# An eight-image convolution, attention and scan program: convolutions placed singly amid two attentions, scans at one pace, last layers three images behind

## The chip, the core and the metric

The kernel runs on one core of a Trainium2 chip. The metric is the device time of one execution in microseconds, the median of several runs. The core's engines each have an instruction queue of their own, worked through in order: TensorE (PE, matrix multiplication), VectorE (DVE), ScalarE (ACT), GpSimd (POOL) and SyncE (SP, which here only issues transfers). PE writes to PSUM, which has eight banks of 512 32-bit columns on 128 partitions; everything else lies in SBUF, and longer-lived data in HBM.

## What is computed

Eight images of 256 channels and 32 x 32 positions, in 32-bit floats, pass through four layers with residual connections, each on normalised input:

```python
x = x + attention(group_norm(x))            # layer 0: 8 heads of 64, l2-normalised q and k
x = x + conv3x3(group_norm(x)) * s1 + b1    # layer 1
x = x + conv3x3(group_norm(x)) + b2         # layer 2
x = x + mixer(group_norm(x))                # layer 3
```

The mixer of layer 3 normalises over channels and sends four groups of 64 channels through a selective scan: a short convolution, projections, then for each of 128 channels and 16 states the recurrence

```python
h = dA_t * h + dBu_t          # 1024 steps
y_t = sum over states of C_t * h
```

Then come a gate, depthwise and pointwise convolutions, a second attention (8 heads of 32), a projection `fc`, layer norms, GELU, a depthwise 3x3 convolution and a last projection. Images don't depend on each other; within an image the layers follow in order.

## The kernel before

A channel takes a partition, so an image is two tiles of 128 x 1024. The program is unrolled Python; each image is cut into pieces that are generators, and what a generator yields is a planned cost. A list scheduler then fixes the order in each engine's queue from the order of the program, from dependencies and from planned durations. Once built, the order doesn't change. PE, DVE and ACT instructions pass through a recording helper, so the profile shows all of them under line L105 and they are told apart by their tiles; POOL's have lines of their own (L974, L1005, L1006).

The pieces of one image:

- *front attention* (`front_attention`): loads x, normalises it (`xn`), makes `v`, `q` and `k`, and works through 64 units. A unit is two score matmuls into a `big` PSUM tile (two banks, two buffers), one exponential on ACT (`p`), and two matmuls of `p` with `v` into `acc`. DVE adds up the `p` tiles (`p<-p`) for the softmax denominators.
- *convolutions* (`front_convs`): the output projection `wout` of the attention, then two times `conv3x3`, 72 matmuls of 512 columns each from the padded images `im`; the result of both halves of a channel tile gathers in one `big` tile. The weights come in 24 transfers of 192 KB (12 for each convolution), issued from ACT's queue into six shared buffers.
- *scan* (`scan_layers`): normalisation, then for each of four groups a front (`branch_front`: projections into the PSUM tile `da`, short convolution on `raw`, step sizes `dt` and `du` written to HBM and read back spread out), 16 units of scan (`scan_steps`) and an end (`branch_back`). A unit is: POOL multiplies `du` by B (`hs<-du,bc`, L974); ACT makes two decays of 512 columns (`da<-dt,a_neg`, one PSUM bank each, two buffers); DVE runs two scans (`hs<-da,hs`); POOL multiplies by C (L1006); PE sums over states (`y<-hs,sel`).
- *back layers* (`back_layers`): the gate, two projections with depthwise convolutions, and the second attention, again 64 units, without DVE's additions. Its results go to HBM as `mix`.
- *ending* (`back_out`, `back_end`): reads `mix`, the projection `fc`, layer norm, GELU, the depthwise convolution (`dw`, 16 DVE instructions), a layer norm, the last projection, and adds the stored `xd`.

A program-level loop sets what runs beside what. Image 0's front attention and convolutions come first, alone. Then round b runs the scan of image b beside the "dense" work: the back layers of b-1, the front attention of b+1, and then the convolutions of b+1 with the ending of b-1 woven in at listed places. Round 0 has no back layers and round 7 no front and no convolutions; after round 7 come back layers and ending of image 7. `interleave` lets the scan take a step each time the dense work's planned cost has passed another `pace`:

```python
    for cost in dense:
        spent += cost or 0.0
        while scans is not None and due <= spent:
            due += pace
            with held():
                if next(scans, END) is END:
```

The pace is 1.8 in round 0, 2.78 in rounds 1 to 6 and 1.6 in round 7. Two steps make a unit of scan. The front attention's costs are multiplied by 0.35 (`slow`), so few scan steps fall into it, and `lull` puts fewer into parts of the convolutions. Under `held()` each scan instruction gets an ordering edge to the last dense instruction of its engine, so the scheduler can't pull it forward. A last block, reached only if a check of the softmax sums fails, computes everything anew by another path; it doesn't run.

Of the kernel before, what the change touches and what calls it, by code (L numbers as in the profile page):

```python
# [19 lines left out]
P = 128  # L20
# [13 lines left out]
def preact_stack(ctx: ExitStack, tc: tile.TileContext, I, out, cols):  # L34
# [16 lines left out]
    ps_acc = ctx.enter_context(tc.tile_pool(name="ps_acc", bufs=1, space=PSUM))  # L51

    xmp = ctx.enter_context(tc.tile_pool(name="xmp", bufs=4))
    mp = ctx.enter_context(tc.tile_pool(name="mp", bufs=3))
    hsp = ctx.enter_context(tc.tile_pool(name="hsp", bufs=6))
    dtp = ctx.enter_context(tc.tile_pool(name="dtp", bufs=2))
    bcp = ctx.enter_context(tc.tile_pool(name="bcp", bufs=4))
    ps_da = ctx.enter_context(tc.tile_pool(name="ps_da", bufs=2, space=PSUM))
# [3 lines left out]
    xdp = ctx.enter_context(tc.tile_pool(name="xdp", bufs=3, space=DRAM))  # L62
# [16 lines left out]
    def xm_tile(name):  # L79
        return xmp.tile([P, TP], F32, tag="xm", name=name)  # L80
# [4 lines left out]
    def tiles(xt):  # L85
        return [xt[:, t] for t in range(2)]

    def load_x(src):
        xt = xp.tile([P, 2, N], F32, tag="x", name="xt")
        nc.sync.dma_start(out=xt, in_=src)  # L90
        return xt
# [146 lines left out]

    images = [wp.tile([P, TW], F32, name="im%d" % t) for t in range(2)]
    raw = wp.tile([P, N + 4], F32, name="raw")  # L240
    for t in images + [raw]:
        nc.gpsimd.memset(t, 0.0)
# [45 lines left out]
    def group_stats(mv, psum):  # L288

        with urgent():  # L290
# [11 lines left out]
            rs = sp.tile([P, 2], F32, tag="rs", name="rs", bufs=4)  # L302
# [4 lines left out]
            shift = sp.tile([P, 2], F32, tag="shift", name="shift", bufs=4)  # L307
# [73 lines left out]
    BY_HALF = tuple((h, da_tile) for h in HALVES)  # L381
# [43 lines left out]

    def project_both(name, srcs, evac):

        last = len(srcs) - 1
        w = [chunk(name, m) for m in range(2)]
        ps = [big_tile() for _ in range(2)]  # L430
        for k, src in enumerate(srcs):
            for m in range(2):
                for h in range(2):
                    tensor.matmul(
                        ps[m][:, HALVES[h]],
                        w[m][:, k],
                        src[:, HALVES[h]],
                        start=k == 0,
                        stop=k == last,
                    )  # L440
                if k == last:
                    evac(m, ps[m])
            yield 4 * 0.86
# [168 lines left out]
    def front_attention(src, img, exact=False):  # L612
        xt = img["x"] = load_x(src)
        yield 0
        mv = stats_tile()
        for t in range(2):
            channel_stats(mv, t, xt[:, t])
        xn = [work("xn0"), work("xn1")]
        group_norm(tiles(xt), group_stats(mv, big_tile), [t[:, 0:N] for t in xn])
# [134 lines left out]
    def conv3x3(xt, mv, name, bname, evac):  # L754
# [4 lines left out]
            tiles(xt), group_stats(mv, acc_tile), [t[:, 1:33, 1:33] for t in im], image  # L759
        )  # L760
        mv = stats_tile()
        for m in range(2):
            scalar.activation(xt[:, m], xt[:, m], AF.Identity, bias=col(bname, m))
        yield 1
        for m in range(2):
            ps = big_tile()
            n = 0
            for c in range(2):
                for dy in range(3):
                    w = chunk(name, (m * 2 + c) * 3 + dy)  # L770
                    for dx in range(3):
                        for h in range(2):
                            tensor.matmul(
                                image(ps[:, HALVES[h]]),
# [5 lines left out]
                        n += 1  # L780
                    if n < 18:
                        yield 5.2
# [5 lines left out]
    def front_convs(img):  # L788
# [19 lines left out]
        def evac_2(m, ps):  # L808
            vector.tensor_add(xt[:, m], xt[:, m], ps)
# [877 lines left out]
```

## Time and profile before

| what | value |
|---|---|
| median of 3 runs | 6551.4 us (6540.02 to 6552.56) |
| the profiled execution, its time | 6534.17 us |
| its span, granted clock | 6532.5 us, 0.91 |
| PE busy | 5503.0 us, 84% |
| DVE busy | 4003.1 us, 61% |
| POOL busy | 2737.3 us, 42% |
| ACT busy | 2701.2 us, 41% |
| convolution matmuls `big<-im,w` | 1104.0 us busy |
| scans `hs<-da,...` on DVE | 1024 instructions, 1265 ns and 1209 ns mean |
| decays `da<-dt,a_neg` on ACT | 1024 instructions, 686 ns mean |
| POOL L974 and L1006 | 512 each, 2636 ns and 2547 ns mean |
| transfers | 495.99 MB, mean 76 GB/s |

A line of a group names what is written and what is read, the shape, the count, busy time and mean, then the engine's idle time just before these instructions and what ended it. A matmul here shows as two records. Lines on waits have the waiting engine and tile, what it waited for, the total in us, the number of waits and the longest. The clock is a share of full speed, as granted to PE.

### The profile page before, as it was taken

What the parts mean: (1) busy time and instruction counts of PE and PEld (TensorE: products, weight loads), DVE (VectorE), ACT (ScalarE), POOL (GpSimd) and SP (SyncE); (2) the same over time, 40 slices, a digit from 0 to 9 for tenths busy, and PEclk for the clock granted to TensorE, in tenths of its full rate; (3) what the DMA queues carried; (4) which work ended last, traced back from release to release, by engine and by line L of the source; (5) the groups of instructions that cost most, each with busy time, mean ns of one, the idle gap of its engine ahead of it and who ended that gap; (6) DMA issues with size and microseconds to landing.
All of it is one profiled execution on the core that took longest, in us unless ns stands there. A gap on an engine that the chain in (4) does not pass through costs nothing.

```text
span 6532.5 us, 52259 instructions
## 1 busy us (share of the span) xinstructions
PE 5503.0 (84%) x17318; PEld 1846.7 (28%) x17318; DVE 4003.1 (61%) x4613; ACT 2701.2 (41%) x3241; POOL 2737.3 (42%) x1302
## 2 busy tenths in 40 slices
PE   8886688899888988989889898899889898876496
PEld 2331133223332233222332233322332223311222
DVE  5247845577556775567756776567855777555622
ACT  3223424644255532644236442555326442344242
POOL 0006653634435353543517345263435435276500
PEclk9997889999899989999899998999899998988697
DMA  1022232323233132321223222231323212233301
GB/s 44 26 62 76 78 89 76 88 74 88 69 91 98 39 93 77 101 85 57 81 82 99 75 75 80 83 103 44 91 77 101 87 57 82 77 82 88 97 26 43
DMA packets 224761, 495.99 MB, mean 76 GB/s; under 512 B 61016, under 2 KB 102616, under 8 KB 223456
## 3 DMA queue, kind: packets, MB, share of 16 engines
q1 hardware_dynamic: 168032, 419.12, 22.2%
q10 hardware_dynamic: 56448, 73.43, 3.9%
q8 instruction: 139, 2.28, 0.1%
q14 instruction: 142, 1.16, 0.1%
HBM read 411.09 MB, written 72.88 MB: 74 GB/s over the span
## 4 chain that ended last, share of the span: by engine, by line
PE 53%; DVE 24%; issue 6%; DMA 6%; ACT 6%; POOL 4%; SPq 1%; ACTq 0%; DVEq 0%; POOLq 0%
PE big L105 33%; PE acc L105 11%; DVE hs L105 6%; PE da L105 5%; DVE p L105 4%; DVE dw L105 3%; POOL hs L1006 3%; PE y L105 3%; DVE u L105 2%; DVE t L105 1%; DMA du_m<-a 1%; POOL hs L974 1%; ACT p L105 1%; ACT da L105 1%; DMA dt<-dt_m 1%
## 5 line engine op out<-in xcount | busy, mean ns | idle before, releaser
L974 POOL TENSOR_TENSOR hs<-du,bc 128x1024 f32<-128x1024 f32 x512 | 1339.7, 2636 | 1623.2 <-DMA du<-du_m 683.0
L1006 POOL TENSOR_TENSOR hs<-hs,bc 128x1024 f32<-128x1024 f32 x512 | 1303.7, 2547 | 1027.7 <-DVE hs L105 841.2
L105 ACT ACTIVATE p<-big 128x1024 f32<-128x1024 f32 x1024 | 1038.5, 1021 | 735.0 <-PE big L105 724.2
L105 PE MATMUL acc<-p,v 128*64 128x512 f32 x4096 | 1151.8, 636 | 8.8 <-ACT both L105 6.0
L105 ACT ACTIVATE da<-dt,a_neg 128x512 f32<-128x512 f32 x1024 | 684.2, 686 | 1144.7 <-DVE hs L105 442.1
L105 PE MATMUL big<-im,w 128*128 128x512 f32 x2304 | 1104.0, 631 | 20.4 <-ACT im L105 20.4
L105 DVE TENSOR_TENSOR p<-p 128x1024 f32<-128x1024 f32 x448 | 720.0, 1607 | 295.2 <-ACT p L105 201.8
L105 DVE TENSOR_TENSOR_SCAN hs<-da,carry,hs 128x512 f32<-128x512 f32 x512 | 623.5, 1265 | 256.4 <-ACT da L105 176.0
L105 DVE TENSOR_TENSOR_SCAN hs<-da,hs 128x512 f32<-128x512 f32 x512 | 599.7, 1209 | 286.6 <-ACT da L105 267.6
L105 PE MATMUL big<-qk,qk 64*128 64x512 f32 x2048 | 647.9, 663 | 95.2 <-ACT p L105 85.5
L105 PE MATMUL y<-hs,sel 128*32 128x512 f32 x2048 | 454.0, 674 | 315.3 <-POOL hs L1006 314.8
L105 PE MATMUL big<-q,k 64*128 64x512 f32 x2048 | 616.8, 660 | 107.2 <-ACT p L105 60.6
L105 PEld LDWEIGHTS big<-im,w 128*128 128x128 f32 x2304 | 446.9, 201 | 689.5 <-issue 642.1
L1005 POOL COPY carry<-hs 128x2 f32<-128x2 f32 x256 | 104.2, 407 | 823.0 <-DVE hs L105 745.0
L105 PEld LDWEIGHTS acc<-p,v 128*64 128x64 f32 x4096 | 213.7, 137 | 820.3 <-issue 719.0
L105 PEld LDWEIGHTS big<-qk,qk 64*128 64x128 f32 x2048 | 178.2, 192 | 537.1 <-issue 280.1
L105 PEld LDWEIGHTS big<-q,k 64*128 64x128 f32 x2048 | 165.8, 190 | 535.5 <-issue 252.6
L105 DVE SCALAR_TENSOR_TENSOR dw<-xo,vec,dw 128x961 f32<-128x961 f32 (+1 forms) x128 | 247.8, 1972 | 16.4 <-ACT dw L105 15.2
L105 PEld LDWEIGHTS y<-hs,sel 128*32 128x32 f32 x2048 | 58.6, 112 | 616.7 <-POOL hs L1006 456.4
L105 PE MATMUL big<-xn,w 128*128 128x512 f32 x512 | 230.1, 601 | 0.0
L105 DVE SCALAR_TENSOR_TENSOR u<-raw,vec,u 128x1024 f32<-128x1024 f32 x96 | 136.2, 1419 | 87.1 <-ACT u L105 85.3
L105 PE MATMUL big<-w,xn 128*128 128x512 f32 x256 | 137.2, 687 | 42.6 <-ACT big L105 34.9
(214 smaller groups left out, 5085.5 us busy)
## 6 DMA issues: line engine op xcount, KB each, us to landing
bc<-bc SPq DMA_DIRECT2D x1024, 128.0 KB
du<-du_m SPq DMA_DIRECT2D x512, 128.0 KB
dt<-dt_m SPq DMA_DIRECT2D x512, 128.0 KB
w<-in_wc ACTq DMA_DIRECT2D x192, 192.0 KB
rs<-inv SPq DMA_DIRECT2D x64, 256.0 KB
dt_m<-dt SPq DMA_DIRECT2D x64, 256.0 KB
du_m<-a SPq DMA_DIRECT2D x64, 256.0 KB
mix<-mix SPq DMA_DIRECT2D x32, 512.0 KB
```

The source lines that it names most:

```text
L105: made = issue(*args, **kwargs)
L974: nc.gpsimd.tensor_mul(u["hs"], u["du"], both_groups(u["bc"][:, 0]))
L1005: nc.gpsimd.tensor_copy(carry[:, u["q"], g : g + 2], hs[:, :, HALF - 1])
L1006: nc.gpsimd.tensor_mul(hs, hs, both_groups(u["bc"][:, 1]))
```

## The change

The rounds are replaced by phases k = -1 to 10. Phase k holds, as "main work", the back layers of image k-3 and then the front attention of image k+1 with the ending of image k-3 woven in; where the front attention has run out (k >= 7) the ending of image k-4 is woven into the back layers. The convolutions of image k form a second stream that advances one step (three matmuls) each time the planned cost of the main work has passed 7.5 (2.9 where a phase has only one attention). The scans of all images form one third stream, with one pace of 1.13 for a step from phase 0 on, held only where the image's convolutions, or the first projection of the back layers two images before, aren't done.

Around this:

- The unit of scan has four steps in place of two: decay and scan of the first half, then of the second, each a step of its own. The PSUM tile `da` has one buffer in place of two; the bank goes to `cv`, a one-bank tile for convolutions, which now work one half of a channel tile at a time, so each weight is loaded twice. The scan's projections and its layer norm go from halves in `da` to whole `big` tiles, shared with the attentions.
- `wout` is taken out of `front_convs` into `front_out`, at the end of the phase before; x is loaded a second time for it. `front_convs` writes `xd` to HBM half by half, and the scan reads it from there into two fixed pairs of tiles (`mixed`).
- `mix` isn't written to HBM; the ending works in three fixed tiles (`room`), and takes `big` for its norms.
- Buffers: `mp` 3 to 2, `hsp` 6 to 5, `bcp` 4 to 3, and POOL's first multiplication is issued one unit ahead (two before).

```diff
-    ps_da = ctx.enter_context(tc.tile_pool(name="ps_da", bufs=2, space=PSUM))
+    ps_da = ctx.enter_context(tc.tile_pool(name="ps_da", bufs=1, space=PSUM))
+    ps_cv = ctx.enter_context(tc.tile_pool(name="ps_cv", bufs=1, space=PSUM))
...
         for m in range(2):
-            ps = big_tile()
-            n = 0
...
+            for h in range(2):
+                ps = cv_tile()
+                n = 0
+                for c in range(2):
+                    for dy in range(3):
+                        w = chunk(name, (m * 2 + c) * 3 + dy)
+                        for dx in range(3):
                             tensor.matmul(
-                                image(ps[:, HALVES[h]]),
+                                image(ps),
...
+                        if n < 18:
+                            yield
+                evac(m, HALVES[h], ps)
...
-        for n in range(-3, len(units) + 2):
-            done = None
-            for ahead, stage in (
-                (3, load), (1, load_dt), (0, decays), (0, None),
-                (0, scan), (-1, weigh), (2, drive),
-            ):
...
+        for n in range(-3, len(units) + 3):
+            at(n + 3, load)
+            at(n + 1, load_dt)
+            at(n, decays, 0)
+            yield
+            at(n, scan, 0)
+            at(n - 1, weigh)
+            done = None
+            if n % 2 == 0 and n >= 4:
+                done = add_up(units[n - 4 : n - 2])
             yield done
+            at(n, decays, 1)
+            yield
+            at(n, scan, 1)
+            at(n + DRIVEN, drive)
+            yield
...
+    AFTER = 3
+    DRIVEN = 1
+    CONVS, CONVS_ALONE = 375.0, 145.0
+    PACE = 1.13
...
+    def main_work(k, convs):
...
+        ending = iter(())
+        if k >= AFTER:
+            img = imgs[k - AFTER]
...
+                ending = ends(k - AFTER - 1) if k > batch - 1 else ending
+            scan_through(k - AFTER)
+            yield from amid(back_layers(img), ending, LATE)
+            ending = ends(k - AFTER)
+        if front is not None:
+            yield from amid(front, ending, ENDING)
+            drain(convs)
+            yield from front_out(imgs[k + 1])
+
+    spent = due = 0.0
+    for k in range(-1, batch + AFTER):
+        convs, n, per = iter(()), 0.0, 1.0
+        if 0 <= k < batch:
+            convs = front_convs(imgs[k])
+            per = (CONVS if AFTER <= k < batch - 1 else CONVS_ALONE) / 50
+        start = spent
+        for cost in main_work(k, convs):
+            spent += cost or 0.0
+            while start + n * per <= spent:
+                n += 1
+                next(convs, None)
+            while due <= spent:
+                with held():
+                    if next(scans, END) is END:
+                        due = spent
+                        break
+                due += PACE
+        drain(convs)
+    drain(ends(batch - 1))
```

## The prediction

> **What bounds the kernel now.** I read the page's slices first, then busy time by stage, then one image's period cut into its parts, then the waits. The slices (40 of 163 us):
>
> ```profile
> PE   8886688899888988989889898899889898876496
> DVE  5247845577556775567756776567855777555622
> POOL 0006653634435353543517345263435435276500
> PEclk9997889999899989999899998999899998988697
> ```
>
> TensorE is the busiest engine, but it is not full. It has holes at slices 4-5 and 36-38, and each hole shows a lower granted clock in the row PEclk. POOL, which works for the scans alone, is empty in the first three slices and the last two. By stage (columns: stretch, its length, busy us and instructions of PE, PE weight loads, DVE, ACT, POOL; then granted clock, DMA share, GB/s):
>
> ```profile
> 0.00:180.00 180.00, 158.90 (x553) 51.84 (x553) 90.54 (x169) 73.61 (x85) 5.42 (x22) 1.00 0.13 40
> 180.00:420.00 240.00, 201.78 (x549) 85.35 (x548) 59.22 (x143) 35.44 (x38) 0.00 (x0) 0.91 0.11 34
> 420.00:1040.00 620.00, 469.69 (x1297) 140.98 (x1298) 402.36 (x414) 229.91 (x296) 350.17 (x160) 0.87 0.28 80
> 1790.00:2540.00 750.00, 662.82 (x2129) 221.30 (x2127) 501.34 (x566) 335.72 (x403) 341.69 (x160) 0.93 0.28 80
> 5570.00:6230.00 660.00, 440.05 (x1301) 140.32 (x1300) 364.50 (x381) 251.48 (x309) 345.69 (x169) 0.80 0.29 83
> 6230.00:6532.00 302.00, 230.18 (x784) 86.91 (x782) 76.00 (x119) 102.78 (x101) 0.00 (x0) 0.86 0.10 33
> ```
>
> In order: front attention of image 0; its convolutions; round b=0 (scan of 0, front of 1); one of the six full rounds, which lie between 1040 and 5570, 755 us each; round b=7 (scan of 7, back of 6); the back layers of 7 alone. The rounds with a scan but only half of the dense work lose most: 470 us of PE in 620, 440 in 660. Inside one full period:
>
> ```profile
> 2275.00:2555.00 280.00, 239.70 (x624) 92.80 (x624) 188.44 (x211) 77.23 (x96) 140.98 (x68) 0.89 0.29 88
> 2555.00:2890.00 335.00, 297.29 (x987) 96.93 (x987) 201.56 (x240) 176.81 (x210) 153.43 (x74) 0.92 0.31 91
> 2890.00:3045.00 155.00, 146.64 (x544) 38.30 (x542) 111.61 (x121) 82.10 (x99) 46.97 (x18) 0.97 0.16 44
> 440.00:770.00 330.00, 238.51 (x745) 59.08 (x744) 250.06 (x216) 148.92 (x191) 201.25 (x84) 0.84 0.30 82
> ```
>
> These are the convolutions with the ending of another image (PE 86% busy at clock 0.89), the back layers (89%), most of the front attention with few scans (95% at 0.97), and, from b=0, a front attention with many scans (72% at 0.84). The convolutions, which need only weights and a buffer, sit where VectorE has the long chains of the ending; the gaps of scan-heavy attention have nothing to fill them. What the engines wait for:
>
> ```profile
> POOL hs L1006 <- DVE hs L105: 841.2, 160, 21.9
> ACT p L105 <- PE big L105: 724.2, 651, 12.4
> DVE hs L105 <- ACT da L105: 443.5, 162, 15.0
> ACT da L105 <- DVE hs L105: 442.1, 322, 22.5
> L105 ACT ACTIVATE p<-big 128x1024 f32<-128x1024 f32 x1024 | 1038.5, 1021 | 735.0 <-PE big L105 724.2
> L105 DVE TENSOR_TENSOR p<-p 128x1024 f32<-128x1024 f32 x448 | 720.0, 1607 | 295.2 <-ACT p L105 201.8
> ```
>
> ScalarE's decay (`da`) and VectorE's scan (`hs`) wait for each other, 442 us each way, and the softmax exponential `p` stands behind a waiting `da` in ScalarE's queue.
>
> **What the Trainium skill says.** "TensorE: Matmul & The Clock Gate", Part 1, says that an activity monitor throttles TensorE's clock after a few idle microseconds and releases it with activity. The trace agrees: 0.98 in 6236 to 6416 us, an attention alone with PE 174.91 of 180 us busy, against 0.68 from 5980 to 6230 with 119.49 of 250. Filling a gap thus pays twice. The same page, "Architectural detail", calls ScalarE and VectorE strict first-in-first-out; the `p` behind a `da` above fits. "GPSIMD Engine Reference", 1. Specifications, says GpSimd shares its SBUF interface with VectorE and that instructions with two SBUF inputs contend. The depthwise group `dw` agrees: mean 1972 ns in the program, 18.43 us for 16 (1.15 us) in the tail, where POOL is idle. "Trainium Kernel Development and Optimization", "Reading a trace", warns that matmul busy time is a poor measure of distance from the limit; so I use busy time only to compare stages of this trace.
>
> **The change part by part.** *Work.* The instruction lists of both programs hold as many matmuls; VectorE loses some two per cent of its instructions and ScalarE, weight loads apart, three. The half-width evacuations of the scan's projections become whole ones and those of the convolutions halves: with 0.6 to 0.75 us for 512 columns and 1.0 to 1.3 for 1024, both signs stay under 10 us an engine. Seven more activation-table loads at 1283 ns: 9 us of ScalarE, hidden, since it is 41% busy. Convolution weights are fetched for each half: 384 transfers of 192 KB for 192, 38 MB on 496; the DMA share goes from about 28% to 31%. They are issued in ScalarE's queue and six buffers hold them, so I cost them at nothing as long as ScalarE isn't stuck; if each step waited one microsecond, 384 us would be exposed, of which some would lie in other gaps. On SP's queue the 64 transfers of `mix` go, and second loads of x, loads of `xm` and 64 more `bc` stores come; the queue's row count rises by two per cent. So nearly everything rests on the placing.
>
> *Prices.* From the stage lines, PE busy: front attention 159, convolutions with `wout` 202, back with ending 230 (of which the ending some 51), a scan 470-159-202 = 109. They add to 700, and a full round shows 663 to 673, since overlapped work is counted once: factor 0.953. VectorE: 91, 59, 76, and 402-150 = 253; sum 479, and 501 to 505 in a full round (POOL stretches it): factor 1.05.
>
> *Where the scans lie.* Counting the steps of the new generators (a scan has 291), phase k (k = -1 to 10) gets of a scan: 0; 0.08; 0.52; 0.52; then 1.23, 1.23, 1.22 and 1.21 in k=3 to 6; 0.51; 0.71; 0.71; 0.07. Image b's scan is done when its back layers begin: only the last 20 steps, at k=10, are run with nothing beside them.
>
> *Phases.* k=-1 as now: 180 with 10 for `wout`, 190. k=0: (159+202) x 0.953 = 344 PE, convolutions filling the attention; at 0.93 busy, between the attention alone (0.97 above) and the convolutions alone (201.78 of 240, 0.84), nearer to the first because the gaps are filled, 370. k=1, 2: with half a scan 398; at 0.91, what 2555 to 3045 shows (444 of 490), 437 each. k=3 to 6: PE (361+230+133) x 0.953 = 690, at 0.91 758. But the front part of the phase carries the attention's additions (91), some 0.63 of the convolutions' share (37), the ending (37, from 6430 to 6532) and, with 59% of the phase's steps, 0.72 of a scan (182) on VectorE: (91+37+37+182) x 1.05 = 364. No slice of this trace has VectorE above 0.81 (132.5 of 163), so I take 0.78: 467. The back part has 295 of PE, at 0.91 324. Together 791 each. k=7: back (179) and convolutions (187 without `wout`) and half a scan (56), 402 after the factor, at 0.91 442. k=8, 9: 293 of PE without convolutions to fill it; 5640 to 5980, with more scans, is 0.77 busy: 380, and 10 for the ending's chains, 390 each. k=10: 219 at 0.9, with 20 for the end of the scan, 265. Then the ending of image 7 alone, as now 102 (6430 to 6532).
>
> The sum: 190+370+874+3164+442+780+265+102 = 6187. The profiled execution took 6534.17 with a span of 6532.5; the median of the runs, 6551.4, is 17 us above it. On that scale the forecast is 6205, 5.3% faster.
>
> *New waits.* `da` has one buffer of 512 for two: ScalarE's second decay waits until VectorE's first scan has read it, and a `p` stands behind it. An image has 128 scans of 512 columns, so 1.22 images in 791 us make one each 5.0 us; the loop da 0.69 + scan 1.24, with one `p` (1.02) and one addition (1.61) queued ahead, is 4.56 us. That is little slack, and I take the wait as inside the 0.78; at best (neither ahead, 1.9 us) it costs nothing, at worst see the slow rival. The scan's projections now take `big`, two buffers that the attention's scores need: some 22 tiles an image at 1 to 3 us, 22 to 66 us, which convolution matmuls may cover; in the 0.91.
>
> **Rivals.** (1) *Even mixing does better*: all stages reach the 95% and 0.97 of 2890 to 3045. For: convolutions never wait for VectorE but for an evacuation each 18 matmuls, many microseconds ahead. Against: that stretch has 18 decays in 155 us, the new phases 31. With 0.95 everywhere and k=8, 9 at 360 the sum is 190+362+838+4x726+423+720+265+102 = 5804; with VectorE at 0.8 in the front parts (455+311 a phase) 5964. I put 5920.
>
> (2) *Slower: the single decay buffer sets the pace.* Place: ScalarE's queue in k=1 to 9, `da` waiting for the scan with `p` behind it, so PE waits for `p`. For: the densities of k=3 to 6 (a whole scan in some 650 us) equal b=0's (one in 620), and there PE was 76% busy although two buffers stood ready. Against: b=0 put its scans into the attention alone and had no convolutions beside it. At 0.76, k=3 to 6 cost 690/0.76 = 908 each, 468 more; with k=1 and 2 at 0.84 (474 each, 74 more): 6205+542 = about 6750. It decides from 876 us a phase (6551 - 6205 spread over four), a scan of 512 columns each 5.6 us.
>
> (3) *Fill and end gain, the middle gives it back*: phases of 875, which is 84 more than above, four times: about 6540.
>
> **How the numbers follow.** Forecast 6205: 0.45; rival 1: 0.22; rival 2: 0.28; rival 3: 0.05. Differences below 0.2%, 13 us, can't be told from none. Faster: 0.45+0.22 and 0.01 of rival 3, 0.68; same 0.02; slower 0.30. The range takes most of rival 1 and some two fifths of rival 2: 5860 to 6700. The likeliest case alone, with 0.74 to 0.82 for VectorE and 0.88 to 0.94 for PE, runs from 6060 to 6360.
>
> **What would show it.** POOL busy from about 540 to 5850 us without peaks; PE near 9 with a clock over 0.9 in the middle; periods near 790 for k=3 to 6; PE 75% busy in k=8 and 9; the last 102 us unchanged. Wrong if ACT's wait for `hs` before `da` grows well past 442 us and PE's share stays at 84%, if PE waits for `w` from memory, or if the middle periods pass 876.

## The result, and the profile after

The changed kernel took 6485.17 us in the median of 4 runs (6477.48 to 6489.31); the kernel before, on the same chip, 6545.71 (6531.35 to 6552.56). The ratio is 0.9909, with a 95% interval of 0.9888 to 0.9930: faster by 0.9%, where 5.3% had been forecast.

The page of the changed kernel (40 slices of 162 us, span 6486.2 us):

```profile
PE   8997997997998789978799787988779977868796
...
DVE  5433776656557685577854977458775456476442
...
POOL 0000454514644366435562646255552456356600
PEclk9998998998999899999899888999899988879897
```

POOL, which works for the scans, is now busy from slice 5 to 38, counted from 1, but still in waves, between 1 and 6 tenths. PE has lost its deep holes at slices 4 and 5. It has shallow ones where one of the first phases passes into the next (7 at slices 4, 7 and 10; these phases, "the fill", run before all kinds of work lie side by side), and in every full phase (7 at 14, 18, 20, 23, 25, 29, 30), and holes near the end remain (6 and 7 at 36, 38 and 40). By phase (columns: stretch, its length, busy us and instructions of PE, PE weight loads, DVE, ACT, POOL; then granted clock, DMA share, GB/s):

```profile
0.00:640.00 640.00, 569.70 (x1764) 195.54 (x1764) 261.53 (x468) 204.83 (x229) 14.65 (x26) 0.95 0.18 51
640.00:1060.00 420.00, 379.88 (x1148) 122.11 (x1148) 293.83 (x321) 169.59 (x208) 203.27 (x91) 0.95 0.34 96
1060.00:1531.00 471.00, 412.11 (x1232) 142.28 (x1232) 278.30 (x364) 171.97 (x205) 168.59 (x79) 0.92 0.26 73
4878.00:5286.00 408.00, 384.61 (x1192) 131.24 (x1190) 202.65 (x225) 174.99 (x199) 169.15 (x86) 0.96 0.35 99
5286.00:5729.00 443.00, 338.17 (x1080) 114.19 (x1080) 263.82 (x285) 202.85 (x231) 216.00 (x107) 0.84 0.28 76
5729.00:6159.00 430.00, 319.86 (x1060) 103.16 (x1060) 267.07 (x260) 194.50 (x229) 270.50 (x128) 0.82 0.31 85
6159.00:6486.00 327.00, 258.66 (x901) 107.58 (x899) 113.55 (x186) 116.89 (x114) 0.00 (x0) 0.84 0.08 25
```

These are k=-1 and 0; 1; 2; 7; 8; 9; and k=10 with the last ending. The first phases and k=7 have PE 88 to 94% busy, k=8 and 9 only 74 to 76% at a clock of 0.82 to 0.84. The four full phases lie between 1531 and 4878. Each is cut in two: the back layers, from the gate of the image to the last score matmul of its second attention, and then the front attention with the ending. The first two phases, back and front in turn:

```profile
1531.00:1838.00 307.00, 282.53 (x932) 88.87 (x934) 195.75 (x182) 152.86 (x181) 185.88 (x93) 0.95 0.39 108
1838.00:2359.00 521.00, 429.23 (x1310) 142.07 (x1308) 365.58 (x429) 214.90 (x254) 240.93 (x108) 0.90 0.28 78
2359.00:2656.00 297.00, 276.53 (x922) 85.30 (x922) 181.80 (x173) 147.30 (x175) 190.47 (x95) 0.97 0.41 114
2656.00:3173.00 517.00, 424.52 (x1316) 141.13 (x1314) 382.40 (x434) 212.15 (x255) 251.53 (x106) 0.91 0.28 78
```

The back parts took 307, 297, 328 and 342 us, with PE 89 to 93% busy at clocks of 0.93 to 0.97. The front parts took 521, 517, 527 and 508 us: PE 80 to 82% at 0.88 to 0.91, VectorE 365.58 to 404.06 us, that is 70 to 77%, 74% in the mean. Neither is full. The chain of waits shows what the time consists of: each piece of it is work or a wait that the next one stood for, and "issue" is time in which an engine waited for nothing that the profile shows. Followed back through a back part and then a front part (share of the stretch by engine and tile, and the number of pieces of the chain):

```profile
by line: PE big L101 27.3%; PE cv L101 15.1%; PE acc L101 13.8%; DVE hs L101 6.7%; DVE u L101 6.3%; issue 5.5%; PE y L101 4.5%; DVE fd L101 2.5%; DVE xm L101 2.3%; DVE dt L101 2.3%; POOL hs L973 1.8%; DVE local L101 1.7%; POOL hs L1001 1.6%
284 pieces in order of time: start us, us, what
```

```profile
by line: PE big L101 15.4%; issue 9.9%; PE cv L101 9.5%; DVE hs L101 8.4%; DVE p L101 7.0%; PE acc L101 4.6%; DVE room L101 3.1%; POOL hs L973 2.8%; DMA rs<-inv 2.7%; PE y L101 2.7%; POOL hs L1001 2.6%; DVE t L101 2.4%; DMA du_m<-a 2.4%; DM
672 pieces in order of time: start us, us, what
```

In the back part PE's four kinds of tile hold 61% of the chain (27.3 + 15.1 + 13.8 + 4.5), in pieces of 307/284 = 1.1 us. In the front part they hold 32% (15.4 + 9.5 + 4.6 + 2.7); the rest passes from engine to engine in pieces of 521/672 = 0.8 us: scans, softmax additions, tiles of the ending (`room`), POOL's products, two round trips through HBM (`rs<-inv`, `du_m<-a`) and "issue". The waits of the whole program that answer to those shown of before:

```profile
ACT da L101 <- DVE hs L101: 1051.7, 555, 19.0
ACT p L101 <- PE big L101: 876.2, 518, 12.1
...
DVE hs L101 <- ACT da L101: 654.1, 411, 17.5
...
POOL hs L1001 <- DVE hs L101: 595.0, 148, 16.7
```

ScalarE's `da` waits 1051.7 us for the scan where it waited 442.1, the scan 654.1 us for `da` (443.5 before), and POOL's second product 595.0 (841.2 before). Three groups (line, engine, operation, tiles, count, busy and mean, idle before and its end):

```profile
L101 ACT ACTIVATE da<-dt,a_neg 128x512 f32<-128x512 f32 x1024 | 706.7, 690 | 1293.1 <-DVE hs L101 1051.7 <-PE cv L101 78.5 <-DMA dt<-dt_m 35.1
...
L101 PE MATMUL cv<-im,w 128*128 128x512 f32 x2304 | 1126.6, 625 | 63.7 <-ACT im L101 36.2 <-DMA w<-in_wc 15.6 <-DVE xt L101 11.8
...
L101 DVE TENSOR_TENSOR p<-p 128x1024 f32<-128x1024 f32 x448 | 713.3, 1592 | 327.8 <-ACT p L101 275.9 <-PE acc L101 42.0 <-DMA sums<-rs 2.9
```

**Where the gain went.** The two ends of the program, k=-1 to 2 and k=7 on, took 6486 - 3347 = 3139 us. They hold four front attentions, four pairs of convolutions, four back layers and 3.1 scans (391 of 1024 scan instructions). Before, 0 to 1040 and 5570 to 6532 with two of the six rounds hold as much, and four scans: 1040 + 962 + 2 x 755 = 3512. So the ends gained 373 us. The four full phases, 3347 us, stand against four rounds, 3020, and gave back 327. Part of both numbers is work that only moved: the ends hold 0.9 of a scan less and the full phases as much more.

### The profile page after: what moved, and what is told of

Read it like the earlier page. It is cut to its first block, busy times and chain, and to the rows that moved or that the text cites. A ratio compares the mean times of both kernels' runs of the same rounds, so it can differ in the third digit from the quotient of the medians.

```text
span 6486.2 us, 52476 instructions
## 1 busy us (share of the span) xinstructions
PE 5516.8 (85%) x17318; PEld 1840.8 (28%) x17318; DVE 3929.3 (61%) x4517; ACT 2678.6 (41%) x3120; POOL 2770.9 (43%) x1302
## 4 chain that ended last, share of the span: by engine, by line
PE 52%; DVE 27%; ACT 6%; issue 6%; DMA 5%; POOL 3%; SPq 1%; ACTq 0%; DVEq 0%; POOLq 0%; another core or an unknown queue 0%
PE big L101 25%; PE cv L101 13%; PE acc L101 10%; DVE hs L101 7%; DVE p L101 4%; DVE u L101 3%; PE y L101 2%; DVE room L101 2%; POOL hs L1001 2%; ACT da L101 2%; DVE t L101 1%; DMA rs<-inv 1%; POOL hs L973 1%; ACT p L101 1%; DVE dt L101 1%
## 5 line engine op out<-in xcount | busy, mean ns | idle before, releaser
L973 POOL TENSOR_TENSOR hs<-du,bc 128x1024 f32<-128x1024 f32 x512 | 1334.0, 2621 | 1813.6 <-DMA du<-du_m 1149.0
L1001 POOL TENSOR_TENSOR hs<-hs,bc 128x1024 f32<-128x1024 f32 x512 | 1310.9, 2561 | 719.8 <-DVE hs L101 595.0
L101 ACT ACTIVATE da<-dt,a_neg 128x512 f32<-128x512 f32 x1024 | 706.7, 690 | 1293.1 <-DVE hs L101 1051.7
L101 PE MATMUL acc<-p,v 128*64 128x512 f32 x4096 | 1201.0, 642 | 27.0 <-ACT p L101 11.1
L101 PE MATMUL cv<-im,w 128*128 128x512 f32 x2304 | 1126.6, 625 | 63.7 <-ACT im L101 36.2
L101 DVE TENSOR_TENSOR p<-p 128x1024 f32<-128x1024 f32 x448 | 713.3, 1592 | 327.8 <-ACT p L101 275.9
L101 DVE TENSOR_TENSOR_SCAN hs<-da,hs 128x512 f32<-128x512 f32 x512 | 622.5, 1216 | 373.6 <-ACT da L101 358.9
L101 DVE TENSOR_TENSOR_SCAN hs<-da,carry,hs 128x512 f32<-128x512 f32 x512 | 653.5, 1276 | 316.3 <-ACT da L101 295.3
L101 PE MATMUL big<-q,k 64*128 64x512 f32 x2048 | 642.9, 690 | 162.5 <-ACT p L101 86.4
L101 PEld LDWEIGHTS cv<-im,w 128*128 128x128 f32 x2304 | 417.2, 194 | 742.0 <-issue 616.8
L101 PE MATMUL y<-hs,sel 128*32 128x512 f32 x2048 | 384.9, 655 | 200.6 <-POOL hs L1001 200.3
L1000 POOL COPY carry<-hs 128x2 f32<-128x2 f32 x256 | 137.1, 536 | 825.7 <-DVE hs L101 735.1
L101 PE MATMUL big<-o,w 128*128 128x512 f32 x384 | 186.1, 632 | 68.2 <-DVE o L101 67.7
L101 DVE SCALAR_TENSOR_TENSOR room<-room,vec,room 128x992 f32<-128x992 f32 (+1 forms) x128 | 200.6, 1567 | 14.0 <-ACT room L101 12.7
L101 DVE SCALAR_TENSOR_TENSOR u<-raw,vec,u 128x1024 f32<-128x1024 f32 x96 | 167.2, 1742 | 60.3 <-ACT u L101 59.2
```

The costliest lines, as they stand in the source:

```text
L101: made = issue(*args, **kwargs)
L973: nc.gpsimd.tensor_mul(u["hs"], u["du"], both_groups(u["bc"][:, 0]))
L1000: nc.gpsimd.tensor_copy(carry[:, u["q"], g : g + 2], hs[:, :, HALF - 1])
L1001: nc.gpsimd.tensor_mul(hs, hs, both_groups(u["bc"][:, 1]))
```

## The experiments

All edits are to the changed kernel, except where the kernel before is named. Ratios are to the kernel before, which has 1; the changed kernel has 0.9909. "Front" and "back" are the parts of k=3 to 6 just measured.

**1. One decay buffer or two.** The single buffer was the slow rival's place. First it was moved to SBUF, with one buffer and with two (the convolution weights then have four buffers for six):

```diff
-    wsp = ctx.enter_context(tc.tile_pool(name="wsp", bufs=6))
+    wsp = ctx.enter_context(tc.tile_pool(name="wsp", bufs=4))
+    dap = ctx.enter_context(tc.tile_pool(name="dap", bufs=1))
...
-            u["da"] = da_tile()
+            u["da"] = dap.tile([P, HALF], F32, tag="das", name="das")
```

> Control for the next run: the changed kernel with its one decay buffer in SBUF in place of PSUM, and four weight buffers in place of six to make room. Decay theory (the single decay buffer makes ScalarE wait and sets the pace of the front parts): about the time of the changed kernel, 6485 us, within 40. VectorE theory (VectorE's bursts of ending, additions and scans set it): the same, or up to 60 slower, since a scan with both inputs in SBUF takes longer.

> As the control, with two decay buffers. Decay theory: ScalarE's 1052 us of waiting for scans falls below 500 and the time falls by 150 us or more against the control. VectorE theory: the waits of ScalarE fall, but the time moves by less than 40 us, because VectorE is what is late.

Measured: 6999.49 us (1.0693, 1.0675 to 1.0711) with one buffer, 6874.33 (1.0498, 1.0480 to 1.0515) with two. Neither expectation held: the first kernel is 514 us slower than the changed one, and the second buffer took ScalarE's wait for scans from 1616.2 us only to 867.8. The pair doesn't answer the question, because the scans themselves grew when their decay came from SBUF (groups of the first kernel; the last section shows when):

```profile
L102 DVE TENSOR_TENSOR_SCAN hs<-das,carry,hs 128x512 f32<-128x512 f32 x512 | 1052.5, 2056 | 268.6 <-ACT das L102 245.7 <-POOL hs L974 20.2 <-issue 2.3
...
L102 DVE TENSOR_TENSOR_SCAN hs<-das,hs 128x512 f32<-128x512 f32 x512 | 931.1, 1818 | 344.1 <-ACT das L102 326.7 <-POOL hs L974 14.1 <-POOL hs L1002 2.8
```

2056 and 1818 ns for 1276 and 1216: (0.780 + 0.602) x 512 = 707 us more of VectorE. Against each other, the second buffer is worth 125 us, but with scans half as long again. The kernel before was then given one PSUM buffer:

```diff
-    ps_da = ctx.enter_context(tc.tile_pool(name="ps_da", bufs=2, space=PSUM))
+    ps_da = ctx.enter_context(tc.tile_pool(name="ps_da", bufs=1, space=PSUM))
```

> The kernel before with one decay buffer in place of two. Decay theory: slower by 150 us or more, in the rounds 0 and 7 above all, where the scans are dense. VectorE theory: slower by less than 60 us.

Measured: 6845.86 us, 1.0464 (1.0447 to 1.0482): 300 us. They do not lie in rounds 0 and 7 above all: of the 308 us by which the span grew, 231 lie in rounds 1 to 6. There a unit issues both decays ahead of both scans, so with one buffer each decay stands right behind a scan; the changed kernel has dense work between its half units. So its own price had to be taken in its own order. A bank for a second buffer comes free when PE's sums over states are left out (the products `hs` are then taken for `y`):

```diff
-                    tensor.matmul(
-                        br["y"][at : at + 32],
-                        sel,
-                        u["hs"][:, e],
...
-    ps_da = ctx.enter_context(tc.tile_pool(name="ps_da", bufs=1, space=PSUM))
+    ps_da = ctx.enter_context(tc.tile_pool(name="ps_da", bufs=2, space=PSUM))
```

> Control for the next run: the changed kernel without the matmuls that sum over the states (1024 of them, 385 us of PE busy time as they stand in the trace); VectorE reads a state tile in their place. It leaves their PSUM bank free. Both theories: 50 to 200 us faster than the changed kernel.

> As the control, with two decay buffers in PSUM. Decay theory: at least 150 us below the control, since one buffer cost the kernel before 300 us and two in SBUF gave 125 back. VectorE theory in its strict form (VectorE's work alone sets the front parts): less than 40 us below. If both hold, some 60 to 150.

Measured: 6299.34 us (0.9632, 0.9608 to 0.9657) with one buffer, 6282.89 (0.9611, 0.9588 to 0.9635) with two: 16 us, and the intervals overlap. The waits of the two, one after the other:

```profile
ACT da L100 <- DVE hs L100: 1090.8, 628, 18.3
...
ACT p L100 <- PE big L100: 727.7, 449, 12.1
...
DVE hs L100 <- ACT da L100: 570.9, 419, 17.2
```

```profile
ACT p L100 <- PE big L100: 913.4, 583, 16.1
...
ACT da L100 <- DVE hs L100: 610.1, 288, 22.6
...
DVE hs L100 <- ACT da L100: 400.0, 177, 16.9
```

The second buffer takes 480.7 us off ScalarE's wait and 170.9 off VectorE's; ScalarE then waits 185.7 more for the scores. The end moves by 16. In this kernel the decay buffer isn't what holds the time, though its wait is one of the longest on the page. That the same holds of the changed kernel, which has the sums and no bank for a second buffer, is suggested but not shown: there the one pair with the sums is that in SBUF, whose longer scans blur it.

**2. Is the spreading of the convolutions worth anything?** They were left to the end of each phase:

```diff
-            while start + n * per <= spent:
-                n += 1
-                next(convs, None)
```

> The changed kernel with the convolutions of a phase run at its end in place of spread through it. All theories: slower. If the spreading is worth what the forecast took (back parts at 0.91 of PE, convolutions in the attention's gaps), by 250 us or more; if VectorE and the decays hold the time anyway, by less than 100.

Measured: 6950.66 us, 1.0634 (1.0612 to 1.0656); the full phases took 932, 915, 921 and 920 us for 828, 814, 855 and 850. Against convolutions in a block at the end of each phase, the spreading is worth 465 us.

**3. Where the ending lies.** In the first kernel only `fc` stays in the front part, and the rest of the ending moves to the back layers of the next phase:

```diff
+            if k > AFTER:
+                ending = ends(k - AFTER - 1) if k > batch - 1 else back_end(imgs[k - AFTER - 1], out[k - AFTER - 1])
...
-            ending = ends(k - AFTER)
+            ending = back_out(imgs[k - AFTER])
```

> The changed kernel with only the projection fc of the ending in the front part of phases 3 to 6 and the rest of the ending in the back part of the next phase. VectorE theory: each front part (now 495 to 530 us) loses 40 to 50 us, each back part (315 to 340) gains 15 to 25: 80 to 140 us less in all, about 6345 to 6405. Decay theory: no more than 30 us either way. Transition theory (the loss is in the chains at phase boundaries): slower by up to 60, since the ending meets the start of the back layers.

Measured: 6413.51 us, 0.9792 (0.9776 to 0.9808), 72 us less than the changed kernel. The front parts fell by about 105 each, to 428, 409, 413 and 402, and the back parts that took the ending rose by 81 to 104, to 399, 409 and 446. With the planned cost of an ending go the scan and convolution steps that it drew along. Phase 3, which has no ending now, is 93 shorter, and k=7, which got one, 82 longer; of the 77 us by which the span fell, 41 come from k=4 to 6 and 23 from k=8 and 9. So an ending, with the steps that it draws along, costs about as much in one attention as in the other. None of the three theories had that: VectorE's came nearest in the sum, but with 40 to 50 us off a front part and 15 to 25 on a back part.

Spreading the ending's steps over the second attention alone:

```diff
-    LATE = [0, 0, 1, 1, 2, 3, 5, 13, 16, 19, 22, 25, 28, 31, 34, 37, 42, 47, 52, 56]
+    LATE = [12, 15, 18, 21, 24, 27, 30, 33, 36, 39, 43, 47, 51, 55, 59, 63, 66]
```

> As ending_late (6414), with the ending's steps placed evenly from the second attention's start on in place of a third of them among the first steps of the back layers, in phases 4 to 10. VectorE theory: the first 100 us of each phase, where VectorE is at 35 of 35 us and PE at 25, lose 10 to 25 us in each of seven phases: 6250 to 6350. Others: within 20 of 6414.

Measured: 6498.55 us, 0.9931 (0.9907 to 0.9954), a miss for both forecasts: 85 us worse than with the steps bunched at the start. k=7 rose from 490 to 511, k=8 from 430 to 456, k=9 from 420 to 440.

The holes of the fill, where one phase passes into the next, are these (stretches of 35 us in the changed kernel):

```profile
560.00:595.00 35.00, 21.22 (x70) 12.74 (x70) 14.13 (x22) 10.09 (x10) 0.00 (x0) 0.57 0.00 0
1015.00:1050.00 35.00, 17.39 (x31) 5.09 (x30) 14.57 (x15) 4.12 (x5) 14.30 (x8) 0.61 0.27 79
1470.00:1505.00 35.00, 17.56 (x40) 6.89 (x37) 6.83 (x11) 1.86 (x3) 11.57 (x5) 0.76 0.47 126
```

PE has 17 to 21 us of work in 35; the chain there, read from 990 to 1110, is the softmax inversion's round trip through HBM, then `wout`, the normalisation of the convolution's input and the first `im`. So loading and normalising the next image was pulled into the end of the phase before, for images 1 to 3:

```diff
+            for n, cost in enumerate(amid(front, ending, ENDING)):
+                yield cost
+                if k + 2 <= AFTER and n in (56, 68):
+                    if n == 56:
+                        begun[k + 2] = front_attention(image_of(k + 2), imgs[k + 2])
+                    next(begun[k + 2])
```

> The changed kernel with the loading and normalising of the next image's front attention pulled into the end of the phase before, for images 1, 2 and 3. Transition theory (chains at the starts of phases 0 to 3, where PE stands 20 to 45 us each, cost some 90 us of the forecast): 25 to 60 us faster. The others: within 10 us.

Measured: 6471.97 us, 0.9896 (0.9874 to 0.9918), 13 less than the changed kernel, with overlapping intervals. k=3 began at 1486 for 1531, but k=3 to 6 took 3382 us for 3347: most of what the fill gained was gone again by k=7.

Three kernels put these together: the spread ending with the early fronts; the same with more of the scan in the back part (pace weighted 1.2 there and 0.83 in the front); and the unspread late ending with the early fronts.

> As ending_spread with the early begin of the fronts of images 1 to 3: another 10 to 20 us less, if the two don't touch the same time.

> As ending_spread_early with the scans at 1.2 of the pace in the back parts of phases 3 to 6 and at 0.83 in the front parts, where VectorE adds up the softmax terms (its p<-p, 90 to 103 us a front part). VectorE theory: 20 to 60 us less again. If one even pace is as good: within 15.

> ending_late with the early begin of the fronts of images 1 to 3. If the two gains add (72 and 13 us): about 6400. If the fill's gain is worth what it was beside ending_spread (57 us): about 6355.

Measured: 6441.85 us (0.9850, 0.9827 to 0.9872), 6588.57 (1.0072, 1.0050 to 1.0095) and 6378.54 (0.9743, 0.9726 to 0.9761). The early fronts, worth 13 us in the changed kernel, gave 57 us beside the spread ending, where 10 to 20 had been expected, and 35 beside the unspread late one, between its two forecasts. In all three pairs k=3 began 39 to 45 us earlier; how much of that reached the end differed, and why is open. The uneven pace was a miss of 147 us: the back parts of k=4 to 6 rose to 495, 481 and 500 from 407, 403 and 424, the front parts fell only to 417, 398, 418 and 376 from 414, 434, 417 and 417. The last of the three is the fastest seen, 2.6% below the kernel before. Its k=3 and k=4, back and front:

```profile
1491.00:1801.00 310.00, 282.45 (x934) 88.45 (x930) 197.83 (x182) 153.62 (x181) 190.32 (x94) 0.95 0.38 106
1801.00:2222.00 421.00, 367.00 (x1176) 122.97 (x1175) 278.27 (x345) 177.49 (x213) 182.87 (x85) 0.94 0.27 77
2222.00:2631.00 409.00, 348.80 (x1098) 113.05 (x1098) 283.63 (x275) 188.37 (x219) 241.79 (x117) 0.90 0.37 105
2631.00:3060.00 429.00, 362.27 (x1146) 118.90 (x1144) 292.47 (x336) 177.62 (x216) 192.47 (x85) 0.90 0.26 73
```

But for the first, which has no ending, its parts are nearly equal, and VectorE has 0.66 to 0.69 of each where the ending or the additions run.

**4. What work in the front part is worth.** Four kernels leave out work: every second depthwise instruction of the ending; the softmax additions; two of the three kernel columns of the convolutions; and these last two together.

```diff
-                vector.scalar_tensor_tensor(
+                n % 2 == 0 or img.get("at") is None or vector.scalar_tensor_tensor(
```

```diff
-                    vector.tensor_add(pair["sum"], pair["sum"], u["p"])
+                    pass
```

```diff
-                            tensor.matmul(
...
+                            if dx == 1:
+                                tensor.matmul(
```

> The changed kernel with every second of the sixteen depthwise instructions of each ending left out (64 of 128, 1567 ns each, so 100 us less of VectorE; nine of them a time in the last, uncovered ending). VectorE theory: 50 to 90 us faster, as the 707 us that decays in SBUF added to VectorE brought 514. If VectorE is not what is late: about 9 us faster, the part in the last ending.

> The changed kernel without VectorE's additions of the softmax terms (448 of 1592 ns, 713 us of VectorE, some 90 to 103 us in each front part). One engine theory, VectorE: the front parts of phases 3 to 6 fall by the additions' whole time, 90 to 100 us each, those of phases 0 to 2 by less than 20. One engine theory, PE: less than 25 us each everywhere. Two-engine theory (both queues wait for each other, each microsecond of either shows in part): 30 to 70 us each in phases 3 to 6; in all 150 to 350 us faster than the changed kernel.

> The changed kernel with one of three columns of the convolution kernels (384 of 1152 matmuls, 750 us of PE busy time less), weights loaded as before. Two-engine theory: front and back parts of phases 3 to 6 both fall, the back parts by most of their share of the convolutions (some 45 us of 60 us each), the front parts by about half of theirs (15 to 30 of 55), the phases 0 to 2, which PE fills at 90% and more, by 60 to 85 us each. VectorE alone: front parts unchanged. PE alone: front parts by 50 or more each.

> Leaves out two parts at once: the softmax additions p<-p (713 us of VectorE) and two of the three kernel columns of each convolution (750 us of TensorE); the weights are still fetched. Each alone gave 191 and 239 us, and in the front parts of k=3 to 6 about 37 and 4 us each. Theory of queues in order (each engine waits for another's single steps, so a piece of work taken out shows in part only and the parts add up): 430 us together, about 6055, front parts about 40 us shorter. Rival, two full engines cover each other (the front part ends when the later of VectorE and TensorE is through, so one alone gives little and both together much): front parts shorter by 80 us or more each, 5900 or less in all.

| kernel | median us | ratio (interval) | start of k=3 | back parts | front parts |
|---|---|---|---|---|---|
| changed kernel | 6485.17 | 0.9909 (0.9888 to 0.9930) | 1531 | 307, 297, 328, 342 | 521, 517, 527, 508 |
| half the depthwise | 6448.53 | 0.9851 (0.9828 to 0.9874) | 1533 | 307, 296, 327, 340 | 514, 515, 535, 500 |
| no additions | 6294.13 | 0.9602 (0.9580 to 0.9623) | 1494 | 307, 297, 326, 345 | 486, 502, 480, 453 |
| a third of the convolutions | 6246.24 | 0.9533 (0.9512 to 0.9553) | 1384 | 301, 290, 316, 318 | 531, 504, 517, 498 |
| both | 5991.09 | 0.9159 (0.9138 to 0.9181) | 1294 | 298, 284, 316, 321 | 503, 463, 463, 453 |

The first front part with the additions left out, the first back and front part with the convolutions cut, and the first two front parts with both:

```profile
1801.00:2287.00 486.00, 412.98 (x1310) 138.58 (x1306) 284.24 (x373) 213.64 (x254) 217.49 (x108) 0.93 0.29 84
```

```profile
1384.00:1685.00 301.00, 256.35 (x850) 77.13 (x850) 199.77 (x201) 156.68 (x184) 181.92 (x93) 0.89 0.39 111
1685.00:2216.00 531.00, 404.52 (x1200) 129.45 (x1198) 368.50 (x410) 210.10 (x251) 236.90 (x107) 0.85 0.27 76
```

```profile
1592.00:2095.00 503.00, 396.25 (x1198) 128.10 (x1194) 277.17 (x354) 209.63 (x250) 222.26 (x108) 0.85 0.28 80
...
2379.00:2842.00 463.00, 383.17 (x1210) 124.85 (x1210) 279.39 (x359) 209.90 (x252) 219.80 (x107) 0.88 0.32 86
```

What a cut took from its engine and what it gave (in the fill, up to the start of k=3, and in the mean of the four back or front parts):

| cut | where | busy us taken | us shorter |
|---|---|---|---|
| additions, from VectorE | fill | 324 | 37 |
| | a front part | 98 | 38 |
| convolutions, from TensorE | fill | 209 | 147 |
| | a back part | 33 | 12 |
| | a front part | 28 | 6 |

The two-engine forecast held for the additions (30 to 70 us a front part) and failed for the convolutions (45 a back part, 15 to 30 a front part). In the fill TensorE's work comes back for the greater part, and in the full phases no cut gave more than two fifths of itself in the mean, not even in the back parts, where PE was 89 to 93% busy. If two full engines covered each other in the front parts, both cuts together would have given 80 us or more of each; they gave 48, where the single ones add to 44. In all they gave 494 us for 430, and most of the surplus lies in the fill (start of k=3 237 us earlier, for 37 + 147). Half the depthwise instructions took 13 us of VectorE from a front part and shortened it by 3; of the 37 us in all some 10 lie in the last ending, which nothing covers. That lies between its two forecasts, 9 us and 50 to 90.

Three things blur these prices. The clock: of the convolutions' own matmuls 679 us went, but PE's busy time fell by only 526, for the others grew longer while the granted clock went from 0.91 to 0.88. POOL: with the additions out its two products fell from 2621 to 2464 and from 2561 to 2458 ns, 33 us less of POOL in a front part, so that cut isn't VectorE's alone. And the order: with instructions gone the scheduler places others anew; with the additions out, at least 164 of VectorE's other 4069 changed places.

With VectorE 55% busy and TensorE 79%, the first front part still took 503 us. Its chain:

```profile
by line: PE big L101 25.2%; PE acc L101 8.2%; DVE hs L101 6.8%; issue 5.9%; POOL hs L1002 5.8%; PE y L101 4.2%; POOL hs L974 4.0%; PE cv L101 3.9%; DMA rs<-inv 2.5%; DVE u L101 2.4%; DMA du_m<-a 2.0%; DMA few<-sums 1.9%; DVE dt L101 1.7%; D
612 pieces in order of time: start us, us, what
```

It is still cut into 612 pieces of 0.8 us. So neither VectorE's work nor TensorE's sets the length of the front part, alone or by covering each other. What is left, and fits the chain, is that steps wait for each other across queues, each worked through in order; that is argued from what remains, and no run takes such a wait away. ScalarE and POOL, 41% and 46 to 58% busy there, weren't unloaded. "Perfetto Trace Analysis", "Identifying the Most-Contended Engine", tells to find the engine with the highest occupancy and to optimise it first, and judges TensorE by its share of the peak rate and by its weight loads (142.07 of 521 us, 0.27, in the first front part) instead of by matmul busy time. By the weight loads that is VectorE in the front parts, at 0.74, and the additions did give more than the convolutions. How much of an engine's work comes back the page doesn't say; here it was 38 of 98 us.

## Why the prediction was wrong in its size

The direction was right, and the place of the gain; the forecast of 6187 us for the profiled execution fell short of the measured span, 6486, by 299:

| phases | forecast us | measured us | difference |
|---|---|---|---|
| k=-1 and 0 | 560 | 640 | +80 |
| k=1, 2 | 874 | 891 | +17 |
| k=3 to 6, back parts | 4 x 324 = 1296 | 1274 | -22 |
| k=3 to 6, front parts | 4 x 467 = 1868 | 2073 | +205 |
| k=7 | 442 | 408 | -34 |
| k=8, 9 | 780 | 873 | +93 |
| k=10 and last ending | 367 | 327 | -40 |

- **The step that failed** is the front part of k=3 to 6: "VectorE (91+37+37+182) x 1.05 = 364", taken at a share of 0.78 as the stage's limit. VectorE's work was 383 us on average (365.58, 382.40, 404.06, 382.06) and its share 0.74. The two errors are small, 25 us each in 518, but the reading behind them is what fell: the stage isn't VectorE divided by a share. Runs showed in its place a stage that follows neither of its two busiest engines: taking 26% of VectorE's work away shortened the front parts by 7%, and its share fell with it, to 0.60. The profile of before had hinted at this: in 440 to 770, quoted in the prediction, VectorE had 0.76 and PE 0.72 at once. There too no engine was full; the prediction used that round, b=0, for its slow rival alone. The chains of its back layers (2555 to 2890) and of that stretch differ as those of back and front parts do, 64% of PE's tiles against some 17%:

```profile
by line: PE big L105 37.7%; PE acc L105 15.1%; PE da L105 8.7%; DMA du_m<-a 4.9%; issue 3.0%; DVE hs L105 2.8%; PE y L105 2.7%; DVE u L105 1.8%; DMA few<-sums 1.8%; DVE p L105 1.7%; DMA bc<-bc 1.6%; DVE dt L105 1.5%; ACT p L105 1.5%; DVE lo
...
by line: DVE p L105 18.2%; issue 14.9%; DVE hs L105 10.1%; PE big L105 7.4%; PE da L105 5.4%; DMA du_m<-a 4.2%; PE acc L105 4.0%; POOL hs L1006 3.2%; DMA dt_m<-dt 2.6%; DMA rs<-inv 2.5%; DVE dt L105 2.5%; POOL hs L974 2.4%; DMA dt<-dt_m 1.9
```

- **The fill** (80 + 17 us): k=-1 took some 225 us for 190, with 202 of PE. The 370 for k=0 were 344 us of PE at 0.93. From 225 to 640, 415 us, PE had 367.24, a share of 0.88: its work was 23 us more, and the rest fits the holes shown above, whose chains were costed at nothing beyond 10 us for `wout`. The early fronts let k=3 begin 39 to 45 us earlier; 13 us reached the end of the changed kernel, 35 and 57 where the ending lay late.
- **k=8 and 9**: the share of 0.77 nearly held (338 of 443 is 0.76, 320 of 430 is 0.74); PE's work was 338 and 320 us for 293, under a clock of 0.82 to 0.84. How much of that the clock made and how much the added prices missed, no run tells apart.
- **Right**: the length of the back parts, as TensorE work at 0.91 (measured 0.89 to 0.93), though as a mechanism it is only in part right, since 33 us taken from PE there gave 12; k=7; the last ending, 109 us from the last product of `p` and `v` to the end for 116 before; the convolution weights, fetched twice for little (the matmuls of `cv` and their weight loads waited 15.6 and 21.0 us for them in the whole program, and ScalarE, which issues them, some 50); ScalarE's seven more table loads; the front part's share of the scans (59%); that the gain rests on the spreading (465 us).
- **The clock**: "Filling a gap thus pays twice" did not show in the whole. The granted clock was 0.91 before and after, and PE's busy time 5503.0 and 5516.8 us; the six full rounds had had 0.92 to 0.94, and the full phases have 0.92 in the mean.
- **Rivals.** "Even mixing does better" came true in k=7, 94% busy and 408 us against its 423; the back parts, 318 us in the mean, lie between its 311 and the 324 of the forecast. "The single decay buffer" had its sign, a wait of 1051.7 us for 442.1, yet its price was 16 us in the pair in PSUM, without the sums, and 125 in that with the long scans; the middle phases, 837 us, stayed below the 876 (791 + 86 is 877) from which it decides. The prediction had named that wait, with a PE share that stays at 84% (it is 85%), as its sign of failure: the sign came, the slowing that it stood for didn't, and the size of the wait was no measure of its price. "Fill and end gain, the middle gives it back", put at 0.05, came nearest in the sum, 6540, and halfway in the cause: the full phases took 837 us each, between the forecast's 791 and its 875. That makes 183 of the 299 us; the other 116 are ends that gained less than it took for granted.

What stays open: which of the waits in the front part carries how much. The pair without the sums over states clears the decay buffer only in a kernel that lacks these sums, and no run took away POOL's products, the inversion's round trip, the order of ScalarE's queue, or the time that VectorE and POOL cost each other (last section) by itself. The runs show that neither VectorE's nor TensorE's work sets the front part, and that small steps remain when both are unloaded; they don't rank those steps.

## What to carry to other kernels

Work spread into gaps was worth its time here, 465 us against the same work in a block. But a stage in which no engine is full can't be forecast by dividing one engine's work by a share: in the full phases a cut gave back a fifth to two fifths of what it took from its engine. Read the chain before the change. Where it passes from engine to engine, as in 440 to 770 of the kernel before, such a forecast is to be given a wide range; where one engine holds most of it, the forecast came true here in length, but a cut still didn't come back in full. A long wait on the page is a price only if its removal moves the end, and the price belongs to one order of the queues: a second decay buffer was worth 300 us in the kernel before and 16 in the new order without the sums. When a schedule is evened out, add up what the ends gain and what the full phases give back separately, with the work that moves between them; here the two nearly cancelled.

## What the runs showed of the hardware

A scan of 512 columns takes 1216 or 1276 ns in the mean with its decay in PSUM, and 1818 or 2056 with it in SBUF. The trace of that second kernel (`da1_sbuf`) tells why, if its scans are sorted by what POOL did at the same time. The 242 and 228 scans that no POOL instruction overlaps took 1216 and 1277 ns, as with PSUM; the 105 and 120 that POOL's work covers from start to end took 2471 and 2686. With the decay in PSUM covered scans took 1217 and 1278 ns: there POOL made no difference. So the whole growth, 707 us of VectorE, comes with POOL working at the same time on scans whose two long inputs both lie in SBUF. POOL pays too: its first product took 2347 ns where VectorE stood idle throughout and 3095 where it was busy throughout.

"GPSIMD Engine Reference", 1. Specifications, says that VectorE instructions with two SBUF inputs contend with GpSimd; the trace agrees. The softmax additions show the same in the changed kernel: 1221 ns where POOL is idle (221 of them), 2248 where it works throughout (100), 1592 in the mean.
